# Layer 3's softmax totals from pairs of source blocks, one chunk behind the values, and elu's sums kept in PSUM

## The chip, the cores and the metric

The kernel runs on one core of one Trainium2 chip. The metric is device microseconds of one execution. The kernel before takes 2933.43 us, the median of 3 runs (2932.90, 2933.43, 2933.43). Engines are named as the profile names them: PE is the matrix engine (PEld its weight loads), DVE the vector engine, ACT the scalar engine, POOL the general engine (GpSimd) and SP the engine that only issues DMAs. Every engine takes its own instructions in a fixed order and stands still at one whose inputs or buffers are not ready.

## The reference, cut to what matters

Sixteen graphs of 1024 nodes with 256 features pass through four attention layers. Each layer normalises, takes a relu and adds its result to `x`:

```python
h = jnp.maximum(_layernorm(x, axis=-1), 0.0)
x = x + _L0_gnn_ref(h, adj, W, a)     # then layers 1, 2 and 3 in the same way
```

A layer projects `h` with a 256 x 256 matrix, makes a weight for each pair of joined nodes from one number of the source and one of the destination, and takes the mean of the projected values under these weights. Layers 1 and 2 end in elu. Layer 3 has four heads of 64 features; each head has its own weights, its own totals (the softmax denominators), and ends in a relu, an addition of the projected values and a normalisation over its 64 features:

```python
attention = jax.nn.softmax(weight, axis=-1)
dst = jnp.einsum('bhij,bhje->bhie', attention, h) + bias[None, :, None, :]
out = jax.nn.relu(dst) + h            # then normalised over each head's 64 features
```

## The kernel before, in words

**Tiling.** A graph's 1024 nodes are eight blocks of 128, one node to a partition. The exponentials are factored, so that the weights of a source block `j` for all 1024 destinations are one DVE instruction: `weigh` (L354) puts the destinations' numbers along a row of PSUM on all partitions (eight transposes at L374, or eight small matmuls at L574 for heads 1 to 3 of layer 3), and then, for each of the eight source blocks, L367 takes the larger or smaller of that row and the block's own number and multiplies by the adjacency mask: 128 x 1024 values in fp32. The row is a single buffer for the whole kernel, so the next row can be written only after the eighth block of weights of the last one is made. The weights have eight buffers for each of two streams.

**Layers 0 to 2.** `attend` (L445) multiplies weights by values on PE (L461): destination block `i` is the sum over eight source blocks, with one more column for the total. The first two destination blocks are summed while the weights are still being made. Two accumulators in PSUM (`accumulator`, L296) take turns. `finish` then adds the result to `x`: for layers 1 and 2 `add_elu` (L388) takes 1/total on DVE, exp and relu on ACT (L393, L395) and two sums on DVE (L396, L397). The accumulator is free when ACT has read it for the relu. As soon as two blocks are done, `project` (L315) normalises, transposes (L338) and multiplies them by the next layer's matrix (L345).

**Layer 3.** For each head, `add_values` (L596) multiplies 32 columns of values at a time, so that four small matmuls (two halves of the destinations, two halves of the head's 64 features) run beside one another in four strips of 32 columns of the array (L586). `add_totals` (L606) does the same with the one column that holds the source block's factor, copied to 32 columns: one group of four small matmuls for two source blocks. A head is done in two chunks of four source blocks; each chunk has four groups of four for the values and two for the totals, and the totals stand before the values of the same chunk. Head 0's values are summed while its weights are made; its totals follow, while head 1's weights are made. After each chunk, the next head's weights of four blocks are made into the buffers that were read. At a head's end ACT copies both accumulators, PE turns them back (L670, L678), DVE takes 1/total and multiplies into `y` (L681), and `center` and `rescale` (L538, L558) do the rest on DVE, ACT and POOL. `y` has one buffer for both streams; the result is stored from `y` by POOL's queue (L704).

**What sets the order.** Two streams (L711) take the even and the odd graphs. Each is a Python generator that yields an estimate of the PE time that it has just issued; the loop at L722 always continues the stream that is behind, and stream 1 starts `LAG = 111.0` later. From this order a scheduler makes each engine's list; some instructions are pinned to the written order. At each copy of an accumulator one more adjacency block is fetched by POOL's queue and squared on ACT (`test`, L165), and one step of the loading of the graph after the next is taken (`load`, L128).

Of the kernel before, what the change touches and what calls it, by code (L numbers as in the profile page):

```python
# [41 lines left out]
P = 128  # L42
# [19 lines left out]
def short_path(ctx: ExitStack, tc: tile.TileContext, ins: dict, out: bass.AP, bad: bass.AP):  # L62
# [131 lines left out]
    def prepare():  # L194
# [45 lines left out]
        for l in range(3):  # L240
            fetch(l)
            yield
            for k in range(NK):
                for s in range(2):
                    prod = work.tile([P, D], F32, name="above", bufs=2)
# [10 lines left out]
        for s in range(2):  # L256
            for k in range(NK):
                prod = work.tile([P, D], F32, name="above", bufs=2)
# [129 lines left out]
    def add_elu(xi: bass.AP, acc: bass.AP, total: bass.AP):  # L388
# [5 lines left out]
        above = work.tile([P, D], F32, name="above", bufs=2)  # L394
        nc.scalar.activation(above, acc[:, :D], AF.Relu, scale=inv)  # L395
        nc.vector.scalar_tensor_tensor(xi, below, 1.0, xi, op0=ALU.min, op1=ALU.add)  # L396
        nc.vector.scalar_tensor_tensor(  # L397
            xi, above, 0.0, xi, op0=ALU.add, op1=ALU.add, accum_out=total
        )

    def batch(b: int):
# [133 lines left out]
        y = single.tile([P, NI, H, E], F32, name="y")  # L535
# [22 lines left out]
        def rescale(yh: bass.AP, blocks, head, rstd: bass.AP, engine=nc.gpsimd):  # L558
            shape = list(yh.shape)
            nc.vector.tensor_mul(yh, yh, rstd.unsqueeze(2).to_broadcast(shape))  # L560
            engine.tensor_mul(yh, yh, gamma[:, head].unsqueeze(1).to_broadcast(shape))
            engine.tensor_add(yh, yh, xb[:, blocks, head])
# [43 lines left out]
        def add_totals(h: int, j: int):  # L606

            parts = [
                (V3[:, j + n, h, E:].to_broadcast([P, QUAD]), halves_of(h, j + n)[g])
                for g, n in ((0, 1), (0, 0), (1, 1), (1, 0))  # L610
            ]
            in_tiles(parts, total, j == 2, j == NI - 4)

        behind = weigh3(0)
        yield from start(behind, b)

# [7 lines left out]
        for h in range(H):  # L624


            acc = accumulator(b)
            total = accumulator(b)
            if h == 0:
                for first in range(0, NI, 4):  # L630
                    for _ in range(4):
                        next(behind)
                    pinned = []
                    for j in (first + 2, first):
                        add_values(h, j)
                    yield 3.6
                for _ in behind:
                    pass
                turned_thirds = psum.tile([3 * QUAD, P], BF, name="misc")
                made = nc.tensor.transpose(  # L640
                    turned_thirds, thirds.rearrange("p t i h -> p (t i h)"), ident_bf
                )
                tc.keep_in_program_order(made)
                thirds_T = small.tile([3 * QUAD, P], BF, name="thirds_T", bufs=1)
                nc.scalar.copy(thirds_T, turned_thirds)
            behind = weigh3(h + 1)
            yield from start(behind, b)

            for first in range(0, NI, 4):
                pinned = []  # L650
                for j in (first + 2, first):
                    add_totals(h, j)
                    if h > 0:
                        add_values(h, j)
                for _ in range(4):
                    next(behind, None)
                yield 1.8 if h == 0 else 5.4
            for _ in behind:
                pass
            copies = []  # L660
            for accT in (acc, total) if h == 0 else (total, acc):
                copies.append(wide.tile([P, HALF], F32, name="sums"))
                nc.scalar.copy(copies[-1], accT)  # L663
                next(testing)
                next(coming, None)
            sums, totals = copies if h == 0 else copies[::-1]
# [20 lines left out]
            if h > 0:  # L687
# [417 lines left out]
```

## Time and profile before

| | |
|---|---|
| median of 3 runs | 2933.43 us |
| the profiled execution's own time | 2933.13 us |
| its span, first to last instruction | 2931.4 us |
| granted clock of PE | 0.995 |
| busy: PE, DVE, ACT, POOL | 2810.0, 2147.9, 1088.2, 981.3 us |
| PE on the products of layers 0 to 2 (L461) | 1435.6 us |
| PE on values and totals of layer 3 (L586) | 691.7 us |
| PE on projections (L345), all forms | 516.1 us in the page's table |
| DVE on weights (L367), both forms | 629.0 and 473.7 us |

The busy time of a group is the union of its instructions' times; the mean of one is longer for small matmuls, which overlap. An fp32 matmul appears as two entries in the counts. "Idle before" is the time for which the engine stood still ahead of the instructions of the group, and the arrow names what ended it.

### The profile page before, as it was taken

How to read it: one execution, taken by the hardware profiler on the slowest of the kernel's cores; microseconds unless marked ns; L12 is line 12 of the kernel's file. 1: busy time of each engine (PE TensorE's matmuls, PEld its weight loads, DVE VectorE, ACT ScalarE, POOL GpSimd, SP SyncE). 2: the span in 40 equal slices, each digit the busy share in tenths (PEclk: the TensorE clock that was granted, in tenths of full speed). 3: DMA queues.
4: the chain of work that ended last, by engine and by line, in shares of the span. 5: the costliest groups of instructions: out<-in, count | busy, mean ns of one | idle time of the engine just before them, and what ended most of it. 6: DMA issues, size and time to landing. Idle time of an engine off the chain costs nothing.

```text
span 2931.4 us, 44756 instructions
## 1 busy us (share of the span) xinstructions
PE 2810.0 (96%) x16790; PEld 1961.9 (67%) x16790; DVE 2147.9 (73%) x4490; ACT 1088.2 (37%) x3010; POOL 981.3 (33%) x1533
## 2 busy tenths in 40 slices
PE   7999999999999999999999999999999999999986
PEld 5775857668576685766758577685766857667552
DVE  5658688586976859778586885868768587685857
ACT  1333434343343433424334343433434334343332
POOL 2123324243242423424233242432424224242333
PEclk9999999999999999999999999999999999999998
DMA  8204022030321303122031220303203031110101
GB/s 126 39 8 65 30 30 58 8 51 29 37 51 16 56 17 51 37 29 59 1 51 37 30 58 8 51 30 37 51 12 47 29 49 39 15 30 1 22 22 31
DMA packets 127967, 106.14 MB, mean 36 GB/s; under 512 B 79872, under 2 KB 98432, under 8 KB 127744
## 3 DMA queue, kind: packets, MB, share of 16 engines
q0 software_dynamic: 47328, 66.10, 15.4%
q1 hardware_dynamic: 79568, 35.53, 5.4%
q8 instruction: 135, 2.21, 0.3%
q10 hardware_dynamic: 848, 1.57, 0.2%
q14 instruction: 88, 0.72, 0.1%
HBM read 153.49 MB, written 33.55 MB: 64 GB/s over the span
## 4 chain that ended last, share of the span: by engine, by line
PE 59%; DVE 26%; issue 8%; POOL 3%; ACT 3%; DMA 0%; POOLq 0%; ACTq 0%; SPq 0%; DVEq 0%
PE acc L461 36%; DVE weights L367 16%; PE acc L586 10%; PE acc L345 9%; PE misc L338 2%; DVE centered L302 2%; POOL rstd L293 2%; DVE V L417 1%; PE row L374 1%; POOL y L544 1%; DVE y L545 1%; DVE var L555 1%; ACT square L309 1%; DVE y L551 1%; DVE mean L549 1%
## 5 line engine op out<-in xcount | busy, mean ns | idle before, releaser
L461 PE MATMUL acc<-V,weights 128*128 128x257 f32 x6144 | 1435.6, 384 | 33.5 <-DVE weights L367 15.7
L461 PEld LDWEIGHTS acc<-V,weights 128*128 128x128 f32 x6144 | 1136.6, 190 | 281.9 <-DVE weights L367 75.3
L586 PE MATMUL acc<-weights,V 128*32 128x512 f32 x6144 | 691.7, 596 | 12.0 <-DVE weights L367 8.1
L367 DVE SCALAR_TENSOR_TENSOR weights<-row,ex,mask 128x1024 f32<-128x1024 f32 x512 | 629.0, 1272 | 97.3 <-PE row L574 65.8
L345 PE MATMUL acc<-W,hT 128*128 128x259 f32 (+1 forms) x2048 | 516.1, 389 | 38.1 <-ACT hT L340 26.9
L367 DVE SCALAR_TENSOR_TENSOR weights<-row,V,mask 128x1024 f32<-128x1024 f32 x384 | 473.7, 1273 | 0.8 <-PE row L374 0.8
L345 PEld LDWEIGHTS acc<-W,hT 128*128 128x128 f32 x2048 | 378.7, 190 | 135.1 <-ACT hT L340 44.4
L586 PEld LDWEIGHTS acc<-weights,V 128*32 128x32 f32 x6144 | 189.1, 110 | 417.7 <-issue 410.3
L393 ACT ACTIVATE below<-acc,inv 128x256 f32<-128x256 f32 x256 | 121.1, 473 | 813.1 <-DVE inv L386 569.6
L293 POOL TENSOR_TENSOR rstd<-rstd,minus_half 128x2 f32<-128x2 f32 (+1 forms) x321 | 292.8, 912 | 20.3
L309 ACT ACTIVATE square<-x_b,minus_mean 128x256 bf16<-128x256 f32 x504 | 255.7, 507 | 110.3 <-DVE minus_mean L332 105.3
L441 POOL TENSOR_TENSOR x_b<-x_b,beta 128x256 f32<-128x256 f32 x128 | 93.5, 731 | 488.6 <-ACT square L309 483.5
L292 POOL TENSOR_SCALAR rstd<-squared 128x2 f32<-128x2 f32 x252 | 80.0, 317 | 464.0 <-ACT square L309 451.0
L385 DVE TENSOR_SCALAR inv<-acc 128x1 f32<-128x1 f32 x256 | 39.1, 153 | 255.3 <-PE acc L461 254.0
L302 DVE TENSOR_SCALAR centered<-x_b,minus_mean 128x256 f32<-128x256 f32 x504 | 195.7, 416 | 5.1
L340 ACT ACTIVATE hT<-misc 128x512 f32<-128x512 f32 x256 | 150.2, 592 | 129.6 <-PE misc L338 129.3
L396 DVE SCALAR_TENSOR_TENSOR x_b<-below,x_b 128x256 f32<-128x256 f32 x256 | 131.8, 515 | 84.9 <-ACT below L393 83.0
L663 ACT COPY sums<-acc 128x512 f32<-128x512 f32 x128 | 74.9, 585 | 308.6 <-PE acc L586 301.0
L413 ACT ACTIVATE V<-acc,rstd 128x3 f32<-128x3 f32 x384 | 98.4, 261 | 231.1 <-PE acc L345 230.6
L417 DVE TENSOR_SCALAR V<-acc,rstd,V 128x256 f32<-128x256 f32 x256 | 131.4, 537 | 59.8 <-ACT V L413 58.9
L338 PE MATMUL misc<-ident,centered 128*128 128x128 f32 x1024 | 158.7, 277 | 13.7 <-DVE centered L325 11.5
L170 POOL DMA_DIRECT2D adj_i<-in_adj_dram x128 | 74.4, 582 | 290.1 <-ACT adj_i L175 248.8
(96 smaller groups left out, 2212.8 us busy)
## 6 DMA issues: line engine op xcount, KB each, us to landing
adj_i<-in_adj_dram POOLq DMA_DIRECT2D x128, 256.0 KB, 3.9
x_b<-in_x_dram SPq DMA_DIRECT2D x15, 1024.0 KB, 6.4
narrow<-in_adj_dram POOLq DMA_DIRECT2D x60, 256.0 KB, 9.3
out_dram<-y POOLq DMA_DIRECT2D x30, 512.0 KB, 7.5
x_b<-in_x_dram ACTq DMA_DIRECT2D x4, 256.0 KB, 6.1
narrow_half<-in_adj_dram POOLq DMA_DIRECT2D x4, 256.0 KB, 16.9
mask<-narrow SPq DMA_TRANSPOSE x60, 3.7
weights<-in_L_gnn_a_dram SPq DMA_DIRECT2D x3, 256.0 KB, 5.5
```

The source lines that it names most:

```text
L293: nc.gpsimd.tensor_tensor(r, r, minus_half.to_broadcast([P, n]), op=ALU.pow)
L302: nc.vector.tensor_scalar(centered[:, n, :], xb[:, 2 * pair + n, :], minus_mean[:, n : n + 1], 0.0, op0=ALU.add, op1=ALU.max,)
L309: nc.scalar.activation(square, xb[:, 2 * pair + n, :], AF.Square, bias=minus_mean[:, n : n + 1], accum_out=squared[:, n : n + 1],)
L338: nc.tensor.transpose(turned[:, k, ts(n, P)], centered[:, n, ts(k, P)], ident)
L340: nc.scalar.mul(hT, turned, ROOT_D)
L345: nc.tensor.matmul(projected, hT[:, k, ts(n, P)], W[l][:, k, :], start=(k == 0), stop=(k == NK - 1),)
L367: nc.vector.scalar_tensor_tensor(w, r, c(j), masks[b][:, j // 2, :, j % 2], op0=op, op1=ALU.mult)
L393: nc.scalar.activation(below, acc[:, :D], AF.Exp, scale=inv)
L396: nc.vector.scalar_tensor_tensor(xi, below, 1.0, xi, op0=ALU.min, op1=ALU.add)
L417: nc.vector.tensor_scalar(V[:, i, :D], projected[:, :D], rstd, V[:, i, D : D + 1], op0=ALU.mult, op1=ALU.mult,)
L461: nc.tensor.matmul(accs[i], weights[j][:, ts(i, P)], V[:, j, : D + 1], start=(j == 0), stop=(j == NI - 1),)
L586: made = nc.tensor.matmul(accT[ts(n, QUAD), :], values, moving, start=first, stop=last)
```

## The change

**Totals by pairs.** `ratio` holds, for each source block and head, the factor of the block before it divided by its own. `add_up` takes two neighbouring source blocks: ACT multiplies the first one's weights by the ratio into a new buffer `added` (128 x 1024), and POOL adds the second one's weights to it. The totals' matmul then has one pass over `added` with the second block's factor in place of two passes over the weights. `added` has two buffers for both streams, which is one chunk.

**A chunk behind.** The totals of a chunk are issued after the values of the next chunk, and those of a head's second chunk after the values of the next head's first chunk. The closing of a head (`close`) moves into the next head's first chunk. The estimates that the streams yield are 2.7 and 2.0 for a chunk in place of 5.4, with the closing's 2.0 between them at a head's first chunk. Head 0's pause of 1.8 for each chunk of its totals stays as a pause in which head 1's weights are made, without the totals. `LAG` is as before.

**elu in PSUM.** The relu is written back into the accumulator, and DVE's first sum is made there too; DVE's second sum adds it to `x`. The accumulator is free after that second sum.

**Buffers.** `above` is gone, and `y` is now the values' own tile `V3`, which is held until the head's end. The last sum of `rescale` writes to `xb`, and the result is stored from `xb`. In `prepare` two scratch tiles take another name.

```diff
@@ add_elu
-        above = work.tile([P, D], F32, name="above", bufs=2)
-        nc.scalar.activation(above, acc[:, :D], AF.Relu, scale=inv)
-        nc.vector.scalar_tensor_tensor(xi, below, 1.0, xi, op0=ALU.min, op1=ALU.add)
+        elu = acc[:, :D]
+        nc.scalar.activation(elu, elu, AF.Relu, scale=inv)
+        nc.vector.scalar_tensor_tensor(elu, below, 1.0, elu, op0=ALU.min, op1=ALU.add)
         nc.vector.scalar_tensor_tensor(
-            xi, above, 0.0, xi, op0=ALU.add, op1=ALU.add, accum_out=total
+            xi, elu, 0.0, xi, op0=ALU.add, op1=ALU.add, accum_out=total
         )
@@ batch, layer 3
-        y = single.tile([P, NI, H, E], F32, name="y")
+        y = V3[:, :, :, :E]
...
-            engine.tensor_add(yh, yh, xb[:, blocks, head])
+            engine.tensor_add(xb[:, blocks, head], yh, xb[:, blocks, head])
...
-        def add_totals(h: int, j: int):
+        added, totals_of = {}, {}
+
+        def add_totals(h: int, first: int):
             parts = [
-                (V3[:, j + n, h, E:].to_broadcast([P, QUAD]), halves_of(h, j + n)[g])
-                for g, n in ((0, 1), (0, 0), (1, 1), (1, 0))
+                (
+                    V3[:, first + 2 * n + 1, h, E:].to_broadcast([P, QUAD]),
+                    added[h, first, n][:, ts(g, HALF)],
+                )
+                for g in range(NH)
+                for n in range(2)
             ]
-            in_tiles(parts, total, j == 2, j == NI - 4)
+            in_tiles(parts, totals_of[h], first == 0, first > 0)
+
+        def add_up(h: int, first: int):
+            for n in range(2):
+                s = added[h, first, n] = single.tile([P, N], F32, name="added", bufs=2)
+                j = first + 2 * n
+                w, w1 = weights[h * NI + j], weights[h * NI + j + 1]
+                nc.scalar.mul(s, w, ratio[:, j + 1, h : h + 1])
+                nc.gpsimd.tensor_add(s, s, w1)
...
+        ratio = ex[:, :, :H]
+        nc.vector.reciprocal(ratio, ratio)
+        nc.gpsimd.tensor_mul(ratio[:, 1:], ratio[:, 1:], V3[:, : NI - 1, :, E])
...
+        closing = iter(())
+        to_add = []
+        for h in range(H):
+            acc = accumulator(b)
+            if h > 0:
+                behind = weigh3(h + 1)
+                yield from start(behind, b)
+            for first in range(0, NI, 4):
+                if h == 0:
+                    for _ in range(4):
+                        next(behind)
+                pinned = []
+                for j in (first + 2, first):
+                    add_values(h, j)
+                if first > 0:
+                    totals_of[h] = accumulator(b)
+                if to_add:
+                    add_totals(*to_add.pop())
+                if first == 0 and h > 0:
+                    closing = close(*to_close)
+                add_up(h, first)
+                to_add.append((h, first))
+                if h > 0:
+                    for _ in range(4):
+                        next(behind, None)
+                    yield 2.7
+                    yield from closing
+                    closing = iter(())
+                    yield 2.0
+                else:
+                    yield 3.6
...
+            sums = copy_of(acc)
+            if h == 0:
...
+                behind = weigh3(1)
+                yield from start(behind, b)
+                for _ in range(2):
+                    for _ in range(4):
+                        next(behind)
+                    yield 1.8
...
+            to_close = h, sums
+        pinned = []
+        add_totals(*to_add.pop())
+        yield from close(*to_close)
...
-                y[:, ts(g, NG)].rearrange("p (c t) h e -> p c t (h e)", t=2),
+                xb[:, ts(g, NG), :].rearrange("p (c t) f -> p c t f", t=2),
```

`copy_of` copies an accumulator to SBUF on ACT and takes the next step of `test` and `load`; `close` holds, in their old order, the turning back, the reciprocal, the product into `y`, `rescale` of the head before and `center` of this one.

More of the change, by code (lines that the diff above doesn't have):

```diff
@@ L244, in prepare @@
                 for s in range(2):
-                    prod = work.tile([P, D], F32, name="above", bufs=2)
+                    prod = work.tile([P, D], F32, name="below", bufs=2)
                     made = nc.vector.tensor_tensor_reduce(
@@ L257, in prepare @@
             for k in range(NK):
-                prod = work.tile([P, D], F32, name="above", bufs=2)
+                prod = work.tile([P, D], F32, name="below", bufs=2)
                 tc.keep_in_program_order(
@@ L623, in batch, with copy_of, close @@
         nc.gpsimd.tensor_sub(thirds[:, 2], rest, thirds[:, 1])
[L624 to L666, printed above, removed]
+        def copy_of(accT: bass.AP) -> bass.AP:
+            copied = wide.tile([P, HALF], F32, name="sums")
+            nc.scalar.copy(copied, accT)
+            next(testing)
+            next(coming, None)
+            return copied
+        def close(h: int, sums: bass.AP):
+            totals = copy_of(totals_of.pop(h))
             yield 0.5
@@ L686, in batch @@
             yield 0.5
-            if h > 0:
+            if normed:
                 rescale(*normed.pop())
@@ L695, in batch @@
             else:
-                normed += [center(h, slice(g * NG, g * NG + NG), nc.vector) for g in range(NH)]
+                normed.extend(
+                    center(h, slice(g * NG, g * NG + NG), nc.vector) for g in range(NH)
+                )
             yield 1.0
+        closing = iter(())
[29 more added lines that the diff above has]
+                    yield 3.6
+            for _ in behind:
+                pass
+            sums = copy_of(acc)
+            if h == 0:
+                turned_thirds = psum.tile([3 * QUAD, P], BF, name="misc")
+                made = nc.tensor.transpose(
+                    turned_thirds, thirds.rearrange("p t i h -> p (t i h)"), ident_bf
+                )
+                tc.keep_in_program_order(made)
+                thirds_T = small.tile([3 * QUAD, P], BF, name="thirds_T", bufs=1)
+                nc.scalar.copy(thirds_T, turned_thirds)
+                behind = weigh3(1)
[4 more added lines that the diff above has]
+                    yield 1.8
+                for _ in behind:
+                    pass
+            to_close = h, sums
+        pinned = []
+        add_totals(*to_add.pop())
+        yield from close(*to_close)
         for _ in coming:
```

## The prediction

> **What bounds the kernel now.** I read the page's busy table first, then one steady graph as a stretch.
>
> ```profile
> PE 2810.0 (96%) x16790; PEld 1961.9 (67%) x16790; DVE 2147.9 (73%) x4490; ACT 1088.2 (37%) x3010; POOL 981.3 (33%) x1533
> ...
> 1484.00:1663.00 179.00, 175.02 (x1053) 122.74 (x1051) 133.45 (x278) 68.17 (x189) 61.75 (x97) 1.00 0.21 36
> ```
>
> The second line is 179 us in mid-run: PE is busy for 175.0 of them, at full clock. PE's idle gaps there recur every 178.5 us, one graph. So PE's own work is the bound, and anything that PE must wait for is paid in full. The timeline of PE and then DVE, where head 0 of layer 3 begins, shows why it hardly waits (start, duration, engine, line, then the idle time before):
>
> ```profile
> 1625.24 1.04 PE L374 MATMUL row<-ident,ex 128*128 128x128 f32 x8
> 1626.12 0.60 PE L338 MATMUL misc<-ident,centered 128*128 128x128 f32 x4
> 1626.56 3.63 PE L461 MATMUL acc<-V,weights 128*128 128x257 f32 x16
> 1630.02 1.04 PE L345 MATMUL acc<-W,hT 128*128 128x259 f32 x4
> 1631.33 3.64 PE L586 MATMUL acc<-weights,V 128*32 128x512 f32 x32 [0.26 <-DVE inverses L385]
> ...
> 1636.03 5.36 PE L586 MATMUL acc<-weights,V 128*32 128x512 f32 x48
> 1641.32 0.62 PE L574 MATMUL row<-thirds_T,rows_of 96*128 96x128 bf16 x8
> ...
> 1626.32 4.86 DVE L367 SCALAR_TENSOR_TENSOR weights<-row,ex,mask 128x1024 f32<-128x1024 f32 x4 [1.80 <-PE row L374]
> ```
>
> From the row's end (1626.28) to the first values (1631.33) lie 5.1 us: DVE needs 4.86 for four blocks of weights. PE fills them with transposes, a product and a projection of the other stream, and idles 0.26. A row is thus a debt: 5.1 us of other PE work must stand behind it. The prices of other PE work come from starts in this view: a product 3.5, one block's projection 0.88, four transposes 0.44, a chunk of 32 + 16 small matmuls 5.29.
>
> **What the Trainium skill says.** "TensorE: Matmul & The Clock Gate", section Architectural detail, has ACT and DVE as strict first-in-first-out queues; the 1.80 us of DVE before the weights agrees in kind. "GPSIMD Engine Reference", section 3.1, has 4497 ns for an fp32 add of 2048 elements, two inputs. "SBUF — State Buffer", section Who interferes with whom: a DVE instruction with two SBUF inputs, or in a two-port mode (tensor_scalar can be), and a POOL instruction reading SBUF block each other for a whole instruction; with one input it doesn't. This fits the instructions of `centered` in the same stretch, a tensor_scalar (minimum/median/maximum ns):
>
> ```profile
> L302 DVE TENSOR_SCALAR centered<-x_b,minus_mean x32: 296/348/1462, 1498.5 to 1637.8; 128x256 f32<-128x256 f32 x32
> ```
>
> **What is removed.** A chunk's totals are 16 of 48 entries, 5.29 x 16/48 = 1.76 us; eight entries remain, so 0.88 goes, eight chunks a graph: 7.05 us a graph, 113 us in all, taken from the bound itself. The order of the changed program confirms one group of four matmuls a chunk in place of two.
>
> **What is added on ACT and POOL.** No row shows these sizes; the nearest are:
>
> ```profile
> L562 POOL TENSOR_TENSOR y<-y,x_b 128x512 f32<-128x512 f32 x63 | 82.4, 1308 | 4.9
> L441 POOL TENSOR_TENSOR x_b<-x_b,beta 128x256 f32<-128x256 f32 x128 | 93.5, 731 | 488.6 <-ACT square L309 483.5
> L553 ACT ACTIVATE wide<-y 128x512 f32<-128x512 f32 x63 | 39.7, 630 | 97.7 <-DVE y L551 97.7
> L553 ACT ACTIVATE wide<-y 128x256 f32<-128x256 f32 x2 | 0.8, 416 | 7.3 <-DVE y L551 6.8 <-DVE var L555 0.5
> ```
>
> POOL: 1308 + 2 x (1308 - 731) = 2.46 us for 1024 elements; half the skill's 4497 is 2.25; I take 2.4. ACT: 630 + 2 x (630 - 416) = 1.06, 1.1 with a pointer scale. There are 256 of each: 280 us on ACT, 615 on POOL. Neither becomes the busiest engine. But from one totals group to the next a chain must run, since `added` holds one chunk: ACT 1.1, POOL 2.4, POOL 2.4 (the second ACT step is hidden), three hand-offs of 0.1: 6.2 us. I summed the PE work that the changed order leaves between consecutive totals groups. The changed order repeats every two graphs (a pair, from here on); before, it repeated every graph. Layer 3's estimates were 4 x 12.8 = 51.2 and are now 10.8 + 3 x 11.4 + 2 = 47.0, and `LAG` still is 111, so the two streams no longer meet in the same places. Of the 14 gaps of a pair inside layer 3, six are too short: 4.2, 4.6, 4.1, 5.1, 5.5, 2.7. Shortfall against 6.2: 2.0 + 1.6 + 2.1 + 1.1 + 0.7 + 3.5 = 11 us a pair, some of it already covered by PE's waits for rows (below), so 8 at least. Followed further, the adds come later still: ACT's multiply stands behind exps and relus whose 1/total waits on DVE; POOL's add behind `gamma` and `bias` steps and a pow of 1.6 us, which wait for DVE's sums, and behind adjacency DMAs (0.58 us of issue each). One case, stream 1's head 2: DVE reaches the head's last weights only when the add before them has ended, the variance sum stands before these weights, the pow and `gamma` follow on POOL, and only then the two adds that the next totals need, 3.6 us late. Adding these by hand down the four lists gives 22. I take 14.
>
> **What is moved: cover.** The moved totals were PE work between rows and values, and the streams' shift changes what stands there. In the changed order, pair of graphs, PE work between a row and its values against 5.1: stream 0, head 0: two projections, 1.8, short 3.3; head 1: half a product and half a pair's projection, 2.6, short 2.5; head 3: seven transposes, 0.8, short 4.3; stream 1, head 0: nothing, short 5.1, and its second chunk another 2.2 (four weights with three elu sums between them on DVE, 6.1, against 3.9). Two rows of layers 1 and 2 have products (7.2 us) at DVE's pace (9.6 for eight weights, with other DVE work), short 2.4 and 2.6. Sum 22.4 us a pair. The same reckoning on the trace of before is 0.85 a graph (0.59 and 0.26 of idle), 1.7 a pair. Net 20.7. These waits follow from PE's fixed order and the 4.86 us alone.
>
> **elu in PSUM.** The accumulator is held for two DVE sums more, about 1 us. What that costs now is small:
>
> ```profile
> PE acc L461 <- ACT above L395: 11.5, 18, 1.6
> ```
>
> One us more on such waits, with L345's, is 1 to 3 us a graph; but L397 can queue on DVE behind a step that waits for POOL's pow. Against that, the first sum had two SBUF inputs and now has one, so by the skill POOL no longer blocks it; `centered` and the normalisation's steps can meet an add of 2.4 us. DVE's weights for the next head now wait for ACT and POOL to have read the old ones, and behind them stand the other stream's `centered`, evictions and elu. An example: in stream 0's head 2 the sum at L547 waits for POOL's `bias` step, which stands behind two adds, a pow and three DMA issues; the head's last weights stand behind L547, and PE's next row behind these: 2 us. For all of these together 0 to 17 us a pair by hand; I take 6, a third, because a wait on PE gives the other engines time to catch up and my walk starts both streams with empty queues.
>
> **Costed at nothing.** `ratio`: a reciprocal and a POOL product of 32 columns, under 0.5 us a graph, hidden in front of the first add; uncovered, 7 us in all. Stores from `xb` and `y` in `V3`: the same two DMAs; a graph's load needs the buffer of three graphs earlier (1 MB lands in 6.4 us), hidden by a graph's 178 us. Copies and adjacency squares: the same number, eight a graph; their queues' delays are counted above.
>
> **Sum.** A pair: -14.1 + 20.7 + 14 + 6 = +26.6 us. Sixteen graphs are seven and a half such pairs, as the ends run with one stream: +200. On the profiled execution (2933.13, span 2931.4 and 1.7 around it; 0.3 below the median) that is 3133. I say 3130.
>
> **Rivals.**
> - *Faster: the cover is there after all.* One mechanism: DVE, busy for 73%, makes each row's weights early enough that PE never starves, and the adds end within their gaps. Place: L586's first values of a head. It then saves 113 and gives some 2820. It decides when new idle stays under 14.1 us a pair; the order puts 20.7 there without any add. 5%; no change (within 0.2%, about what a measurement of this kernel can tell) 3%.
> - *Slower, by rows alone.* The adds hide in the waits for rows: -14.1 + 20.7 = 6.6 a pair, 50 in all, 2983. For it: POOL and ACT are busy for 33% and 37%. Against: six gaps below 6.2 us. 17%.
> - *POOL's chain becomes the bound in layer 3.* The hand sums in full, 22 and 17: +45.6 a pair, 3275, or more if idle stretches of 5 us lower PE's granted clock (one page of before has no such loss: its mean is 0.995). 15%.
> - That the change doesn't halve the totals is ruled out by the order.
>
> **How the numbers follow.** My case (rows, adds and queues, 3020 to 3240) has 60%. The range of 80% goes from the rows-only 2985 to 3275, which the bounds of adds (8 to 22) and queues (0 to 17) span: 2933 + 7.5 x (6.6 + 8) = 3043 and 3275 are their ends, the rows-only case its lower one. Slower in sum 92%.
>
> **What would show it.** L586's entries fall from 6144 to 5120 and its busy time by some 110 us. PE's busy total falls to near 2700 while the span grows. PE's waits for DVE's weights at L588 grow to over 100 us, PE's waits for POOL's add (L629) to about 100, DVE's for POOL appear at L367. An add should take 2.4 us and a multiply 1.1. If PE idles under 8 us a graph, the prediction is wrong, and the row debts were met.

## The result: 3361.85 us, and the profile after

The changed kernel takes 3361.85 us (median of 4 runs, 3360.57 to 3362.17) against 2933.43: a ratio of 1.146, 95% interval 1.144 to 1.148. The direction was forecast, the size was not: 3130 had been said, 3275 at most.

The page of the changed kernel, its busy row and its row of the granted clock over 40 slices:

```profile
PE 2901.4 (86%) x15766; PEld 1978.0 (59%) x15766; DVE 2294.2 (68%) x4506; ACT 1368.0 (41%) x3266; POOL 1544.2 (46%) x1805
...
PEclk9998999999899999999999999999998999999997
```

PE has 1024 fewer entries than before, and yet is busy for 91.4 us longer; its idle time in the span of 3360.3 has gone from 121 to 459 us. The mean granted clock is 0.947 (before 0.995). In the clock row this is nearly invisible, since a slice is 84 us long and nearly all drops are 3.4 or 6.8 us: few digits show an 8.

The groups' rows (busy and mean ns after the first bar):

```profile
L629 POOL TENSOR_TENSOR added<-added,weights 128x1024 f32<-128x1024 f32 x256 | 606.5, 2386 | 265.7 <-ACT added L628 207.9
L588 PE MATMUL acc<-weights,V 128*32 128x512 f32 x4096 | 539.7, 674 | 140.7 <-DVE weights L367 95.0 <-POOL added L629 39.2 <-ACT sums L649 3.6
L628 ACT ACTIVATE added<-weights,ex 128x1024 f32<-128x1024 f32 x256 | 284.2, 1142 | 260.0 <-PE acc L588 170.3
L588 PE MATMUL acc<-added,V 128*32 128x512 f32 x1024 | 188.3, 621 | 77.1 <-POOL added L629 74.5
```

An add takes 2.386 us and a multiply 1.142, as estimated (2.4 and 1.1), and the entries of the totals are halved. Waits of PE, the three longest and one for the row's own buffer:

```profile
PE acc L588 <- POOL added L629: 113.7, 66, 5.4
PE acc L588 <- DVE weights L367: 95.0, 27, 8.0
PE acc L345 <- DVE inv L385: 37.4, 9, 4.8
PE row L576 <- DVE weights L367: 26.7, 10, 3.7
```

The columns are total us, times and the longest. The two that were forecast stand at the head, but the first must be read with the groups' rows: of its 113.7 us only 74.5 lie ahead of totals. The other 39.2 lie ahead of values, which do not read `added`. DVE's fourth block of weights ended 0.15 us before each of these values, as it does before most other waits for weights, and the run without adds below has the same wait of 5.36 us once a pair. So they are waits for weights that the view puts down to an add ending at the same time: 134 us for weights, 74.5 for adds.

One steady pair of graphs of each kernel as a stretch (length, then busy time of PE, PEld, DVE, ACT, POOL, the clock, the DMA share and GB/s), before and after:

```profile
1484.70:1841.70 357.00, 349.03 (x2098) 244.98 (x2098) 266.33 (x553) 136.34 (x378) 123.00 (x191) 1.00 0.21 36
```

```profile
1161.90:1571.30 409.40, 361.75 (x1971) 247.41 (x1970) 285.57 (x554) 171.49 (x410) 193.09 (x224) 0.95 0.20 32
```

A pair is 52.4 us longer. PE's idle time in it grew by 39.7 us, from 8.0 to 47.7: the prediction's 20.7 + 14 + 6 = 40.7. What it did not have is the rest: PE should be busy for 349.0 - 14.1 = 334.9 us and is busy for 361.8. A wait in the timeline of this pair shows where that comes from (start, duration, engine, line, and the idle time before):

```profile
1497.55 0.60 PE L668 MATMUL misc<-ident,sums 128*128 128x128 f32 x4
1502.42 6.37 PE L588 MATMUL acc<-weights,V 128*32 128x512 f32 x32 [4.27 <-DVE weights L367]
1508.60 1.04 PE L588 MATMUL acc<-added,V 128*32 128x512 f32 x8
...
1497.42 4.86 DVE L367 SCALAR_TENSOR_TENSOR weights<-row,ex,mask 128x1024 f32<-128x1024 f32 x4
```

This is a row debt as the prediction drew it: the row ends, DVE needs 4.86 us for four blocks, PE stands still for 4.27. But the 32 entries that follow then take 6.37 us, where the same 32 took 3.64 before. The same stretch in three windows (columns as above):

```profile
1497.70:1501.10 3.40, 0.45 (x5) 0.21 (x2) 3.40 (x4) 2.47 (x6) 1.97 (x3) 1.00 0.01 2
1501.10:1507.90 6.80, 5.48 (x28) 1.60 (x32) 6.60 (x17) 1.20 (x4) 2.27 (x3) 0.50 0.25 39
1507.90:1511.30 3.40, 3.40 (x24) 1.81 (x17) 3.40 (x5) 1.54 (x2) 0.32 (x1) 0.99 0.00 0
```

PE's clock was granted in full while PE stood still, and then fell to 0.50 for 6.8 us just as work came. The wait cost 4.27 us and then 2.73 more. The clock record of the trace has 70 such drops in the changed kernel, 359 us in all; the kernel before has 3, all at its very end.

### The profile page after: what moved, and what is told of

Its sections match the earlier page's. It is cut to its first block, busy times and chain, and to the rows that moved or that the text cites. A ratio compares the mean times of both kernels' runs of the same rounds, so it can differ in the third digit from the quotient of the medians.

```text
span 3360.3 us, 43234 instructions
## 1 busy us (share of the span) xinstructions
PE 2901.4 (86%) x15766; PEld 1978.0 (59%) x15766; DVE 2294.2 (68%) x4506; ACT 1368.0 (41%) x3266; POOL 1544.2 (46%) x1805
## 3 DMA queue, kind: packets, MB, share of 16 engines
q0 software_dynamic: 47328, 66.10, 13.8%
## 4 chain that ended last, share of the span: by engine, by line
PE 45%; DVE 29%; POOL 14%; issue 7%; ACT 4%; DMA 1%; POOLq 0%; ACTq 0%; SPq 0%; DVEq 0%
PE acc L462 27%; DVE weights L367 16%; PE acc L345 9%; POOL added L629 7%; PE acc L588 6%; POOL rstd L293 3%; PE misc L338 2%; DVE V L553 2%; POOL V L546 2%; DVE V L562 1%; DVE centered L302 1%; DVE var L557 1%; DVE V L547 1%; DVE mean L551 1%; ACT added L628 1%
## 5 line engine op out<-in xcount | busy, mean ns | idle before, releaser
L462 PE MATMUL acc<-V,weights 128*128 128x257 f32 x6144 | 1451.7, 387 | 52.8 <-DVE weights L367 30.5
L462 PEld LDWEIGHTS acc<-V,weights 128*128 128x128 f32 x6144 | 1144.4, 192 | 301.1 <-DVE weights L367 100.2
L629 POOL TENSOR_TENSOR added<-added,weights 128x1024 f32<-128x1024 f32 x256 | 606.5, 2386 | 265.7 <-ACT added L628 207.9
L367 DVE SCALAR_TENSOR_TENSOR weights<-row,ex,mask 128x1024 f32<-128x1024 f32 x512 | 631.6, 1275 | 88.6 <-POOL added L629 32.3
L588 PE MATMUL acc<-weights,V 128*32 128x512 f32 x4096 | 539.7, 674 | 140.7 <-DVE weights L367 95.0
L345 PE MATMUL acc<-W,hT 128*128 128x259 f32 (+1 forms) x2048 | 561.5, 411 | 99.3 <-DVE inv L385 37.4
L345 PEld LDWEIGHTS acc<-W,hT 128*128 128x128 f32 x2048 | 390.7, 201 | 230.9 <-issue 112.4
L588 PEld LDWEIGHTS acc<-weights,V 128*32 128x32 f32 x4096 | 137.4, 122 | 468.0 <-issue 384.7
L628 ACT ACTIVATE added<-weights,ex 128x1024 f32<-128x1024 f32 x256 | 284.2, 1142 | 260.0 <-PE acc L588 170.3
L292 POOL TENSOR_SCALAR rstd<-squared 128x2 f32<-128x2 f32 x252 | 50.7, 201 | 499.0 <-ACT square L309 485.4
L588 PE MATMUL acc<-added,V 128*32 128x512 f32 x1024 | 188.3, 621 | 77.1 <-POOL added L629 74.5
L385 DVE TENSOR_SCALAR inv<-acc 128x1 f32<-128x1 f32 x256 | 38.6, 154 | 304.8 <-PE acc L462 302.6
L302 DVE TENSOR_SCALAR centered<-x_b,minus_mean 128x256 f32<-128x256 f32 x504 | 242.9, 521 | 3.5
L397 DVE SCALAR_TENSOR_TENSOR acc<-below,acc 128x256 f32<-128x256 f32 x256 | 107.8, 427 | 121.3 <-ACT acc L396 120.9
L338 PE MATMUL misc<-ident,centered 128*128 128x128 f32 x1024 | 158.0, 277 | 22.1 <-DVE centered L325 11.5
```

The source lines that it names most:

```text
L302: nc.vector.tensor_scalar(centered[:, n, :], xb[:, 2 * pair + n, :], minus_mean[:, n : n + 1], 0.0, op0=ALU.add, op1=ALU.max,)
L338: nc.tensor.transpose(turned[:, k, ts(n, P)], centered[:, n, ts(k, P)], ident)
L345: nc.tensor.matmul(projected, hT[:, k, ts(n, P)], W[l][:, k, :], start=(k == 0), stop=(k == NK - 1),)
L367: nc.vector.scalar_tensor_tensor(w, r, c(j), masks[b][:, j // 2, :, j % 2], op0=op, op1=ALU.mult)
L462: nc.tensor.matmul(accs[i], weights[j][:, ts(i, P)], V[:, j, : D + 1], start=(j == 0), stop=(j == NI - 1),)
L588: made = nc.tensor.matmul(accT[ts(n, QUAD), :], values, moving, start=first, stop=last)
```

## The experiments

The readings to be told apart: that the granted clock, falling after idle stretches, is the missing part (the theory); against it, that elu's sums in PSUM slow the matmuls, or that the adds or the rows alone account for everything. From here on, "a pair" is the mean of four pairs of graphs in mid-run, counted from the trace; "at half clock" is the time in it at a granted clock of 0.5. Lines that an edit puts in move the line numbers of its run by one to three, in the pauses by up to eleven.

| kernel | us | ratio, 95% interval | a pair, us | PE idle | at half clock |
|---|---|---|---|---|---|
| before | 2933.4 | 1 | 357.0 | 8.0 | 0 |
| changed | 3361.9 | 1.146 (1.144 to 1.148) | 409.6 | 48.5 | 41.8 |
| changed, PE's gaps filled | 3439.7 | 1.172 (1.170 to 1.174) | 419.6 | 47.2 | 40.1 |
| before, short pauses | 3204.0 | 1.092 (1.090 to 1.094) | 391.4 | 27.8 | 21.3 |
| before, long pauses | 3345.0 | 1.140 (1.138 to 1.142) | 409.6 | 41.6 | 41.0 |
| changed, no adds | 3082.7 | 1.051 (1.049 to 1.052) | 375.5 | 29.9 | 23.9 |
| changed, adds unread, one buffer | 3250.2 | 1.108 (1.107 to 1.110) | 394.2 | 41.7 | 41.0 |
| changed, adds unread, two buffers | 3217.6 | 1.097 (1.095 to 1.099) | 393.6 | 39.1 | 40.1 |
| changed, old elu | 3369.3 | 1.148 (1.146 to 1.150) | 413.0 | 51.3 | 35.0 |
| before, elu in PSUM | 3055.9 | 1.042 (1.040 to 1.044) | 372.0 | 18.2 | 10.2 |
| before, estimates 47.0 | 3017.4 | 1.028 (1.027 to 1.030) | 368.6 | 18.5 | 7.7 |
| before, estimates and elu | 3124.2 | 1.065 (1.063 to 1.066) | 382.3 | 30.1 | 17.1 |
| changed, lag 134 | 3305.5 | 1.127 (1.125 to 1.128) | 401.9 | 47.9 | 38.4 |
| changed, no adds, lag 134 | 3022.7 | 1.030 (1.029 to 1.032) | 365.1 | 24.5 | 16.2 |
| before, lag 136 | 3002.5 | 1.023 (1.021 to 1.025) | 365.0 | 14.3 | 6.0 |
| before, elu in PSUM, lag 136 | 3024.0 | 1.031 (1.030 to 1.033) | 367.2 | 15.8 | 4.3 |

### The clock: filling PE's gaps

```diff
+    FILL = {(0, 0): 6, (0, 1): 4, (0, 3): 8, (1, 0): 10}
...
+                if first == 0:
+                    for _ in range(FILL.get((b % 2, h), 0)):
+                        idle = nc.tensor.matmul(
+                            acc[:, :D], ident, W[0][:, 0, :D], start=True, stop=True
+                        )
+                        tc.keep_in_program_order(idle)
                 for j in (first + 2, first):
                     add_values(h, j)
```

`FILL` is by stream and head.

> The changed kernel with 448 needless 128 x 256 matmuls (0.44 us each) put behind a row and ahead of the first values, at the four places of a pair of graphs where the order leaves TensorE without work: 28 a pair, 12.3 us of work into 15.2 us of waiting. Theory (an idle stretch of some 3 us or more is followed by a stretch of 3.4 or 6.8 us at half clock, and that is the part of the loss that the waits themselves do not explain): the idle time there turns into busy time and costs nothing, and three or four of the six or seven half-clock stretches of a pair go, 1.7 to 3.4 us each: 3270 to 3315 us, mean clock at least 0.96. Rival (the matmuls are slower for another reason, PSUM or port contention by elu's sums, or the clock follows the mean load of TensorE rather than single idle stretches): 3355 to 3375, clock still 0.947.

Measured: 3439.7 us, 78 slower than the changed kernel. Neither theory said so. PE's waits of this run:

```profile
PE acc L589 <- POOL added L630: 78.6, 67, 3.2
PE acc L463 <- DVE x_b L399: 56.9, 17, 5.9
PE row L577 <- DVE inverses L386: 49.9, 7, 7.1
```

The waits for weights at the values are gone from the head of the list, as meant, but 57 us of waits for elu's results (13.8 before the edit) and 50 for 1/total ahead of a row (none of note before) have come in their place. PE's idle time in a pair is hardly changed (47.2 for 48.5), the dummies came on top (PE is busy for 11 us more), and the time at half clock hardly moved. An idle stretch of PE was thus not free room to be filled. A likely reason, not tested apart: DVE itself waits for PE (its waits for PE's products at L385 are 302.6 us in the changed kernel), so work put into one gap makes a later result late. As a test of the clock this run settles nothing, since the idle time didn't go.

### The clock: pauses put into the kernel before

```diff
+                if h > 0 and first == 0:
+                    with tc.high_priority():
+                        for n in range(2):
+                            probe = psum.tile([P, D], F32, name="misc")
+                            made = nc.tensor.matmul(probe, ident, bias, start=True, stop=True)
+                            tc.keep_in_program_order(made)
+                            for _ in range(4 if n == 0 else 0):
+                                nc.gpsimd.tensor_mul(bias, bias, ones.to_broadcast([P, D]))
+                    held = [made]
```

The second run has 8 in place of 4. The next chunk's matmuls are kept behind the second probe.

> The kernel before, with a pause of TensorE put in after the first chunk of heads 1 to 3 of every graph, 48 in all: a needless 128 x 256 matmul, then 4 multiplies by one on POOL (0.73 us each, in place, on a vector that the matmul has read), then a second matmul that waits for them; 0.6 to 2 us of other work stand between. This dose is meant to leave 1 to 2.4 us of idle time, under the length at which the clock was seen to fall: 42 us of matmuls and 50 to 115 of idle time, 3025 to 3090 us, at most a dozen half-clock stretches. Rival (any idle time costs clock): above 3100 with 40 or more stretches.

> The same with 8 multiplies: 2.9 us more for each pause, 4 to 5.3 us of idle time. Theory (an idle stretch of 3 us or more is followed by 3.4 or 6.8 us at half clock, 1.7 to 3.4 us lost): above the smaller dose by 48 x 2.9 = 140 for the longer pauses and by 80 to 165 for the clock, 220 to 300 us in all, with 40 to 60 half-clock stretches. Rival (single pauses cost only themselves): 120 to 160 above, few stretches.

PE's waits in the two runs, short and long:

```profile
PE misc L661 <- POOL bias L664: 150.2, 48, 6.0
```

```profile
PE misc L661 <- POOL bias L664: 262.7, 48, 8.1
```

Both expectations missed in their numbers: 3204.0 and 3345.0 us. The short pauses were not as short as meant, 3.1 us in the mean and up to 6.0, because POOL often came late to them; the run has 36 drops of the clock, the one with the long pauses 50. So the step between the doses is only 141 us: 112.5 of longer waits, and 28 for 14 more drops, 2 us each. This lies in the range of the rival that gave the clock no part (120 to 160), but it had few drops, and here the smaller dose already has most of them.

What settles the question is each run's own sum. The short pauses cost 271 us, the long ones 412. PE's idle time grew by 157 and 265 us, and the dummies take 42 by estimate (96 at 0.44); 72 and 104 us are neither. PE worked at half clock for 138 and 210 us more than in the kernel before, and if half of that is lost, it is 69 and 105. In a kernel that is otherwise untouched, waits of PE thus cost four to five tenths more than they last. And the single pauses show which of them do it: of the short run's, none of the 16 under 1.5 us was followed by a drop, and all 32 of 2.2 to 6.0 us were; of the long run's, 46 of 48.

What sets off a drop can be read from the clock records of 15 runs (all but the kernel before). In each, the drops begin on a fixed grid of 3.4133 us. This is the count of windows by PE's busy share in the window just before, a run's first and last few left out:

```
busy share of the last window   windows   next one at half clock
last one at full clock:  under 0.40    507      506
                         0.40 to 0.55  343      111
                         over 0.55   11966        1
last one at half clock:  under 0.75    329      329
                         0.75 to 0.85   75       45
                         over 0.85     573        0
```

"TensorE: Matmul & The Clock Gate", section What's actually happening, of the Trainium skill gives the window, 3413 ns and free-running, and the trace agrees. Its section HAM oscillation puts the rule as no idle gaps over some 3.4 us. Here the measurement is stricter: it was enough that PE was idle for six tenths of a window. In the changed kernel 47 of its 51 idle stretches of 3 us or more were followed by a drop, 2 of 12 between 2 and 2.5 us; whether a shorter one does it depends on where the grid cuts it and on other idle time beside it. And once down, the clock came back only after a window with PE busy for over 0.75, which is why a drop often lasts for two.

### The adds: left out, and made but not read

```diff
-                s = added[h, first, n] = single.tile([P, N], F32, name="added", bufs=2)
-                j = first + 2 * n
-                w, w1 = weights[h * NI + j], weights[h * NI + j + 1]
-                nc.scalar.mul(s, w, ratio[:, j + 1, h : h + 1])
-                nc.gpsimd.tensor_add(s, s, w1)
+                added[h, first, n] = filled
```

`filled` is a constant tile of ones. The unread adds keep the multiply and the add, into a tile `s` of their own with one buffer, then with two.

> The changed kernel without the multiplies and adds: the totals' matmuls read a constant tile, so the totals are not the reference's; TensorE's order and the number of its matmuls stay. Theory (rows first, adds second, the clock on top of both): the waits for the adds and what they delay on DVE go, 20 to 25 us a pair, and with them two or three half-clock stretches; the row waits of 20 us a pair and their half-clock stretches stay: 3060 to 3190 us, clock about 0.97. Rival 1 (the adds alone make the loss): about 2820 to 2850. Rival 2 (the rows alone make it): above 3280.

> As the run without adds, but ACT and POOL make all the adds, into a buffer that nothing else reads, while the totals read the constant tile: TensorE never waits for an add, ACT's and POOL's queues and the SBUF port have all of their work. Theory: the queues' part is small, so 0 to 70 us above the run without adds. Rival (the adds cost by standing in the queues and by blocking DVE, not by being waited for): within 60 us of the changed kernel's 3362.

> The unread adds again, now with two buffers for them, as in the changed kernel, so that ACT's multiply need not wait for the add before it; the totals read a constant tile. Theory (in the run with one buffer ACT's copies of the sums stood behind multiplies that waited for POOL: 12 us a pair of idle time and its clock; the mere presence of the adds costs little): 3085 to 3160 us. Rival (queues and port cost as such): 3220 or above.

Measured: 3082.7 us without adds, as the theory said, so the adds cost 279 us in all. Without them the idle time of a pair is 21.9 us above before; the prediction had 20.7 for the rows. The main wait:

```profile
PE acc L590 <- DVE weights L369: 131.5, 35, 6.2
```

The unread adds missed: 3250.2 us, and 3217.6 with two buffers, where the rival had named 3220 or above, so that 135 of the 279 us come although no total waits for an add. One buffer was a flaw of the first of these runs: ACT stood 280 us at the next multiply until POOL was done, with the copies of the sums behind it. With two, the trace shows two causes. One is seen on DVE, two groups of the run without adds and then of that with two buffers:

```profile
L304 DVE TENSOR_SCALAR centered<-x_b,minus_mean 128x256 f32<-128x256 f32 x504 | 177.0, 392 | 3.1
L564 DVE TENSOR_TENSOR V<-V,rstd 128x512 f32<-128x512 f32 (+1 forms) x65 | 44.9, 691 | 72.4 <-POOL rstd L295 72.4
```

```profile
L304 DVE TENSOR_SCALAR centered<-x_b,minus_mean 128x256 f32<-128x256 f32 x504 | 251.2, 538 | 4.3 <-PE misc L340 1.1
L564 DVE TENSOR_TENSOR V<-V,rstd 128x512 f32<-128x512 f32 (+1 forms) x65 | 75.8, 1167 | 78.0 <-POOL rstd L295 78.0
```

The same instructions of DVE last longer: 392 to 538 ns, 691 to 1167. DVE's busy time goes from 2109.7 to 2282.6 us with the same 4507 instructions. The weights, which take one input from PSUM, stay at 1.27 us, and elu's sums at 0.43. The trace ties this to the adds: in the run with two buffers, a `centered` that starts while an add runs lasts 1975 ns in the mean (42 of the 504), one that meets no instruction of POOL 345 (213 of them), and one that starts during a multiply on ACT with no add running 326 (17). This is what the Trainium skill describes in "SBUF — State Buffer", section Who interferes with whom. The other cause is seen in the queues: the copies of the sums stand on ACT behind multiplies that wait for weights, and PE's waits for these copies grow from 19 to 63 us, 44 of the 82 us by which PE's idle time grows between the two runs. DVE's next weights must also wait until the adds have read the old ones, but that is 1.4 us here; in the changed kernel it is 52 (32.3 for POOL, 19.5 for ACT). How the 135 us divide between the two causes was not measured apart.

The remaining 144 us come when the totals read the adds and wait for them. One such wait of the changed kernel, on PE and on POOL:

```profile
1344.26 1.05 PE L588 MATMUL acc<-added,V 128*32 128x512 f32 x2 [1.80 <-POOL added L629]
1345.23 0.71 PE L345 MATMUL acc<-W,hT 128*128 128x259 f32 x2
1347.71 1.06 PE L588 MATMUL acc<-added,V 128*32 128x512 f32 x6 [1.77 <-POOL added L629]
...
1341.85 2.35 POOL L629 TENSOR_TENSOR added<-added,weights 128x1024 f32<-128x1024 f32 x1
1344.17 1.14 POOL L546 TENSOR_TENSOR V<-V,bias 128x512 f32<-128x512 f32 x1
1345.26 2.39 POOL L629 TENSOR_TENSOR added<-added,weights 128x1024 f32<-128x1024 f32 x1
```

A `bias` step stands between the two adds on POOL. PE waits for the first, runs one strip of the group alone (two entries, 1.05 us) and a piece of a projection, and waits again for the second; the other six entries then take 1.06, as long as all eight otherwise. 39 of the 128 groups are broken like this. The 0.9 us of the lone strip is counted as busy, but it is a wait in another form: in a pair the totals occupy PE for 20.6 us, against 14.0 in the run without adds. As 2.4 of the 20.6 run at half clock, which makes 1.2, 5.4 are left for the broken groups.

### Elu's sums and the estimates

Elu's edit, as the change has it, put on the kernel before (and taken out of the changed kernel):

```diff
-        above = work.tile([P, D], F32, name="above", bufs=2)
-        nc.scalar.activation(above, acc[:, :D], AF.Relu, scale=inv)
+        elu = acc[:, :D]
+        nc.scalar.activation(elu, elu, AF.Relu, scale=inv)
-        nc.vector.scalar_tensor_tensor(xi, below, 1.0, xi, op0=ALU.min, op1=ALU.add)
+        nc.vector.scalar_tensor_tensor(elu, below, 1.0, elu, op0=ALU.min, op1=ALU.add)
...
-            xi, above, 0.0, xi, op0=ALU.add, op1=ALU.add, accum_out=total
+            xi, elu, 0.0, xi, op0=ALU.add, op1=ALU.add, accum_out=total
```

The lower estimates, put on the kernel before alone and with elu's edit:

```diff
-                yield 1.8 if h == 0 else 5.4
+                yield 1.8 if h == 0 else 4.7
```

> The kernel before with only elu's sums put in PSUM. Theory (this part is small: an accumulator held for 1 us more, and an order that leaves 7 us a pair more of uncovered rows): 0 to 80 us slower, 2933 to 3013. Rival (elu's sums in PSUM make the matmuls or DVE slower throughout): 3050 or above, with TensorE's busy time up by over 50.

> The changed kernel with elu's relu and sums back in SBUF. Theory (the sums in PSUM hold the accumulators, 4.5 us a pair of graphs in the changed kernel's trace, and they shift the order: 24 us a pair of uncovered rows are left in place of 31): 8 to 11 us a pair of waits go and 2 to 5 of clock with them: 3245 to 3290 us. Rival (elu's place plays no part, the adds and the lag do): 3340 to 3380.

> The kernel before with nothing changed but the planner's estimate of a chunk of heads 1 to 3 of layer 3, 5.4 to 4.7, so that layer 3 counts 47.0 in place of 51.2 as in the changed kernel. The work is the same to the instruction, only the streams' interleaving moves. Theory (the lower estimates with an unchanged lag uncover rows: by the order 17.6 us a pair of graphs in place of 8.2): 9 us a pair of new idle time and 3 to 5 of clock: 3000 to 3060 us. Rival (the estimates don't matter, elu and the adds do): 2925 to 2960.

> The same with elu's sums in PSUM as well; whole totals, no adds. Theory (estimates and elu together are what uncovers the rows in the changed kernel: the order leaves 33 us a pair of them, against 31 there): 20 to 25 us a pair of new idle time and 8 to 14 of clock, 3140 to 3230 us; that is the run without adds (3083) with the 106 us of the removed totals given back. Rival (the rows in the changed kernel lose their cover through the moved totals): 3050 to 3090, little above the run with elu alone.

Measured: estimates alone 3017.4 us (within what was expected), elu in PSUM alone 3055.9 (above its 0 to 80, in the range of its rival), both together 3124.2 (just below the range); the changed kernel with the old elu 3369.3, no gain at all where 70 to 115 us had been expected, as its rival had it. The rival of elu alone, slower matmuls, does not hold all the same: PE's busy time rose by 39 us, where it had over 50, and 35 of them are half of the 71 us more that PE works at half clock. PE's waits with elu alone, and with both:

```profile
PE acc L586 <- DVE weights L367: 83.2, 18, 5.0
```

```profile
PE acc L586 <- DVE weights L367: 146.8, 46, 5.4
```

Estimates and elu each alone put 10 us of idle time into a pair, together 22, and most of it at weights after a row (the kernel before has 8.1 us in the place of the two lines). That is the run without adds again (21.9), though here the totals are whole and in their old place. So the rows lose their cover through the interleaving of the streams, which the estimates shift and elu's sums in PSUM shift as well; PE's instructions in the run with the estimates alone are the same ones as before. Taking elu out of the changed kernel only exchanges one interleaving for another: its waits for `x_b` and for 1/total go, others of the same size for `hT`, `above` and `centered` come.

### Another pairing of the streams

```diff
-    LAG = 111.0
+    LAG = 134.0
```

In the two runs on the kernel before it is 136.

> The changed kernel with the second stream 134 instead of 111 behind, all else the same: the same work is paired in another way, and the order now leaves 11 us a pair of uncovered rows instead of 31. Theory: 20 us a pair of waits go, 150 in all, and with them about four half-clock stretches a pair, 60 to 110 us: 3050 to 3170 us, clock 0.97 or more. Rival (the adds or elu's sums make the loss, wherever the streams meet): 3290 or above.

> The run without adds (3083 us), with the second stream 134 behind instead of 111; the totals are not the reference's. Theory (what is left there are rows without cover, and the order of this pairing leaves 6 us a pair of them in place of 28): idle time under 12 us a pair, few half-clock stretches, 2830 to 2910 us, below the kernel before. Rival (what TensorE waits for is DVE's own pace, which no pairing mends, as the same shift with the adds in place gained only 56 us): 3000 or above.

> The kernel before with the second stream 136 instead of 111 behind. Theory (uncovered rows fall from 8 to under 1 us a pair of graphs by the order; against that the ends, where one stream runs alone, grow by 25 each): idle time in mid-run of 3 to 6 us a pair, 2900 to 2945 us in all. Rival (a shift of the streams costs as it does in the changed kernel, through DVE's lateness elsewhere): 2960 or above.

> The kernel before with elu's sums in PSUM and the second stream 136 behind. Theory (elu in PSUM alone cost 122 us because the order with it leaves a row of each graph without cover, 5.2 us twice a pair, and this pairing leaves 2 us a pair): within 40 us of the run with the same lag and the old elu. Rival (holding the accumulators costs wherever the streams meet): 60 to 130 us above that run.

In the first three the time lay in the rival's range: 3305.5, 3022.7 and 3002.5 us. PE's waits in the changed kernel with a lag of 134:

```profile
PE acc L588 <- POOL added L629: 115.2, 63, 4.6
PE acc L462 <- DVE x_b L398: 52.5, 16, 8.0
```

The waits for weights at the values fell from 134 to 49 us (counted as above, with those put down to adds), as the order had it. Others grew by about as much: for the adds at totals from 74.5 to 89, for elu's results (L462 and L345) from 36 to 55, for the row's own buffer (L374) from 5 to 28, for `centered` from 9 to 26, for `hT` from 19 to 31. Without adds, elu's results alone are waited for 70 us at this lag. The kernel before, shifted so that the order leaves almost no uncovered row, idles for 14.3 us a pair in place of 8.0, above all for `centered` (5.1). Counting the work behind rows thus says which way the waits at rows go, but does not choose the best order: it leaves out what else DVE is late with. The fourth run held: with the lag of 136, elu in PSUM costs 21 us, not 122, so its price is that of the interleaving it meets. No version here beats the kernel before.

## Why the prediction was wrong

- **What bounds the kernel, what is removed, the prices.** Right. A multiply takes 1.142 us, an add 2.386, and the totals have half their entries.
- **Moved cover, 20.7 us a pair.** The mechanism came as said, a little smaller: PE's waits for weights at values and products are 1.7 us a pair before, 17.8 in the run without adds and 19.1 in the changed kernel, so 16 to 17 new ones. That the whole idle time without adds grew by 21.9 looks closer and is in part luck: the rest are waits for copies of the sums (2.4), elu's results (1.7) and others. The reason was half of it: the prediction named the estimates with an unchanged lag, and elu's sums, which it had under queues alone, shift the interleaving as much (10.5 and 10.2 us a pair alone, 22.1 together). That the moved totals were the cover is not shown by any run: the same idle time came with the totals in their old place.
- **Adds and queues, 14 + 6 us a pair.** PE's idle time ahead of totals is 8.7 us a pair. With the 5.4 of broken groups, which count as busy time, that is the 14 that had been taken. The queues were put too small: the rest of the new idle time is some 14 us a pair for 6, most of it at 1/total (4.7), elu's results (4.5), the row's own buffer (4.0) and smaller ones. The 135 of the adds' 279 us that come although no total waits for them say the same. The share of longer DVE instructions in it is open.
- **The sum.** Here it failed. New idle time was 40.5 us a pair where 40.7 had been summed; with terms of 17, 9 and 14 for 20.7, 14 and 6, that this total fits is luck. But the sum let an idle microsecond of PE cost one microsecond, and took -14.1 from busy time at full clock. Half clock costs a pair 18.3 us (half of the 36.6 us that PE works at it), and the broken groups 5.4. With these, -14.1 + 40.5 + 18.3 + 5.4 = 50.1 of the 52.6 us measured; 2.5 are not assigned. Times seven and a half pairs the 52.6 are 394.5 us of the 428; the other 34 lie outside these pairs, at the ends, and were not followed.
- **The rivals.** "Rows alone" would have been 2983; the run that has them alone took 3083. Its pair is some 12 us longer than summed: 9 of them are half of the 17.9 us that PE works at half clock, 1.2 are more idle time. "POOL's chain in full" carried the words that idle stretches of 5 us may lower PE's clock, as an extra to one rival with 15%. It belonged to every case that had new idle time, the prediction's own too. The page of before was no evidence against it: no idle stretch in mid-run is over 1.7 us there, and its mean of 0.995 is itself such a loss. It comes from three drops at the end (half of 30 us, in a span of 2931), one at each of the only three idle stretches of over 2.5 us after the start. One of the three in the trace of before, and the window that follows (columns as in the stretches above, the clock third from the end):

```profile
2853.03 9.46 PE L586 MATMUL acc<-weights,V 128*32 128x512 f32 x60 [5.04 <-DVE weights L367]
...
2851.90:2858.80 6.90, 5.77 (x28) 1.58 (x32) 5.75 (x5) 0.00 (x0) 0.00 (x0) 0.51 0.00 0
```

- **What would show it.** The entries of values and totals (4096 + 1024 = 5120) came as said, and so did waits for weights (134 us, over 100 said) and for adds (74.5, about 100 said). But the busy time of these entries did not fall by some 110 us, it rose from 691.7 to 728, and PE's busy total did not fall to near 2700, it rose to 2901: this line of the page, with the mean clock of 0.947, is where the failing step is seen first.

## What to carry to other kernels

When a change leaves PE with idle stretches of some 2.5 to 6 us, add to each about 2 us for the window or two at half clock that follow; small gaps, which left PE busy for over 0.55 of a window of 3.4 us, cost only themselves here. Look for such stretches at the ends of the trace that you already have. Work taken from the busiest engine is worth little if the engines that take it over also feed that engine: the totals' 106 us were gained, and the adds cost 279, half of it though no total waited for them. And where an order is planned from estimates, a lower estimate is a change of its own: 5.4 to 4.7 in one line cost 84 us with the very same instructions.

## What the runs showed of the hardware

- In these runs the granted clock of each window of 3.4133 us followed from PE's busy share in the one before: at full clock it fell after 506 of 507 windows under 0.40 and after 1 of 11966 over 0.55; at half clock it stayed down after 329 of 329 windows under 0.75 and rose after 573 of 573 over 0.85.
- 128 x 1024 adds on POOL, a fifth of the run, stretch DVE's instructions on SBUF by 37% (`centered`, 392 to 538 ns) to 69% (a 128 x 512 product of two inputs, 691 to 1167 ns) in the mean. A `centered` that starts while an add runs lasts 1975 ns, one that meets nothing on POOL 345; weights and elu's sums, with an input from PSUM, stay as they were (1.27 and 0.43 us).
- Filling 12.3 of 15.2 us of expected waits a pair with needless matmuls made the kernel 78 us slower and left the idle time nearly as it was (48.5 to 47.2 us a pair).
